# A transformer block on one core: banks per copying engine at the beginning, weights by another queue, bias additions and last transposes in other slots

## The chip, the cores and the metric

The kernel runs on one core of a Trainium2 chip. The metric is the device time of one execution in microseconds (us). A core has TensorE (matmuls and transposes), VectorE, ScalarE, GpSimd and SyncE; each works through its own list of instructions in order, and they wait for each other by semaphores. DMAs are issued from the list of an engine (here SyncE's and ScalarE's) and carried out by 16 DMA engines. TensorE writes to PSUM[...]; the other engines copy results from there into SBUF.

## The reference

A transformer block in float32 on x of 2 × 1024 × 256 with a context of 2 × 154 × 192:

```python
h = _layernorm(x, ln1_g, ln1_b)
x = _attention(h, h, sa_wq, sa_wk, sa_wv, sa_wo, sa_bo) + x        # 16 heads of 64
h = _layernorm(x, ln2_g, ln2_b)
x = _attention(h, cond_emb, ca_wq, ca_wk, ca_wv, ca_wo, ca_bo) + x
h = _layernorm(x, ln3_g, ln3_b)
p = h @ ff_w1 + ff_b1
a, gate = (p[..., :D_FF], p[..., D_FF:])                            # D_FF = 1024
h = a * jax.nn.gelu(gate, approximate=False) @ ff_w2 + ff_b2
return h + x
```

`_attention` projects queries, keys and values with heads side by side, takes the softmax of q·k/8 along the keys, weighs the values with it, and multiplies by the output weights, with the bias added.

## The kernel before, in words

**Stages.** The 16 heads are taken in 8 pairs, so there are 16 units of (batch, pair). After a beginning the work is written out by hand as a row of slots: 128 self-attention slots (loop at L991, variable `p`, 8 per unit), 48 cross-attention slots (loop at L1012, variable `c`, 3 per unit), and 64 slots of the gated feed-forward. No planner moves anything: each engine gets its instructions in the order in which the loops emit them.

**A self-attention slot** takes 128 query rows for both heads of the pair. `self_first` computes two tiles of scores (L445, 16 matmuls each) into PSUM, VectorE takes their maxima (L606), ScalarE the exponents (L456, four instructions). The keys of a row lie in two halves on different partitions, so maxima and sums of the halves are exchanged: `exchange` issues four DMAs of 1 KB from SyncE's queue (L466). In the next slot, `join` (L474 to L482) lets GpSimd and ScalarE put the halves together, VectorE takes the reciprocal (L553), and GpSimd scales the exponents (L557, four instructions). `turn_groups` (L571) lets VectorE transpose them, two slots after their scores.

**What lies beside it in a slot.** In order: the scores, stored copies from the slot before, exponents, transposes, additions of output tiles (`adds`), the scaling, one entry of the list `later` (L1009: loads of x, of weights, single bias additions on GpSimd at L288), `load_ahead` (L640: weight slices for the unit after next), and then TensorE work. Slots 0, 1, 4 and 5 of a unit take this from `run_work`: the projections of queries, keys and values of the next unit (L330, L355), output tiles (L423), norm pieces. Slots 2, 3, 6 and 7 multiply values (`self_values`, L492).

**PSUM** has three pools: two buffers of two banks for scores, two single banks (`mm_tile`) for projections and output tiles, and two single banks for sums (`sum_tile`).

**The beginning** (L944 to L980) normalises the first batch in four pairs of row tiles: statistics on VectorE, the power −0.5 on GpSimd (L220), the normalisation on ScalarE (L240, two per pair), four transposes of a pair into one bank (L247), and four copies out of it with gain and shift. For pairs one and three VectorE makes all copies (L257), for pairs two and four VectorE makes two and ScalarE two (L261). Queries and keys of the first unit are projected in halves of two pairs each, and ScalarE copies them (L340, L344). Ahead of and between these TensorE transposes the identity into an unused bank 32, 10 and 4 times (L959).

**Weight slices.** `load_slice` (L123) issues them on SyncE's queue: a slice of queries, keys or values of self-attention is two DMAs of 128 KB. `load_ahead` asks for them in slots 2 (queries), 3 (keys) and 7 (values) of a unit, in unit 0 in slots 5, 6 and 7. Of the cross-attention's weights it loads the first.

**Bias additions.** `add_biases` puts eight additions and one load into `later`, at the start of units 4 and 6 for the self-attention's bias, so that each of eight slots from slot 0 on takes one.

**Output tiles.** `out_piece` (L418) multiplies 128 rows of one half of the pairs (four matmuls) and VectorE adds the result to x (L430). From unit 4 on, two such tiles are due in each unit, in an order that takes tiles 3 and 7 last; those of batch 1, first half, are due in units 12 to 15.

**The end of self-attention.** `self_drain` (L654) runs in cross slots 0 to 4: the scaling of slot 127 in slot 0, the transposes of slots 126 and 127 in cross slots 0 and 1. The values of the last slots are multiplied in cross slots 3 and 4. A cross slot computes scores (L733), their maxima on VectorE (L738), exponents on ScalarE (L749), scaling on GpSimd (L760) and transposes on VectorE (L776).

Of the kernel before, what the change touches and what calls it, by code (L numbers as in the profile page):

```python
# [13 lines left out]
P = 128  # L14
# [4 lines left out]
def tile_transformer_block(ctx: ExitStack, tc: tile.TileContext, a: dict, out: bass.AP):  # L19
# [103 lines left out]
    def load_slice(name, c0, n, p):  # L123

        own = w[name][:, c0:c0 + n]
        if p != HR:
            return load_rows(wpool, name[3:], f"{name}_{c0}", own, p)
        t = wpool.tile([P, NH, n], F32, tag=name[3:], name=f"{name}_{c0}")
        for r0 in range(0, P, HR):
            nc.sync.dma_start(out=t[r0:r0 + HR], in_=own.rearrange("(c p) f -> p c f", p=HR))  # L130
        return t
# [3 lines left out]
    def load_weights(kind, pr, what):  # L135
        if kind == "sa" or what == "q" or what == "k":
            wsl[kind, pr, what] = load_slice(
                f"{kind}_w{what}", pr * P, P, HR if kind == "sa" or what == "q" else CC)
        elif pr % 2 == 0:
            wsl[kind, pr, what] = load_slice(f"{kind}_w{what}", pr * P, VC, CC)  # L140
# [50 lines left out]
    def norm_pieces(kind, b, first=False):  # L191
# [31 lines left out]
        def normalize(t):  # L223
# [9 lines left out]
            for i in range(2):  # L233
                xs = xt[b, order[t + i] // GT][:, order[t + i] % GT, :]
                xs, own = xs.rearrange("p (c d) -> p c d", c=nh), xn[:, :, i, :]
                if kind == "ca" and not narrow(kind, b):
# [6 lines left out]
        def turn(t):  # L243
            ph = spare["bank"](f"ph_{ln}_{b}_{t}").rearrange("p (c k) -> p c k", c=nh)
            for i in range(2 * D // P):

                nc.tensor.transpose(  # L247
                    ph.rearrange("p c k -> p (c k)")[:, i * P:(i + 1) * P],
                    st["xn", t].rearrange("p c i d -> p (c i d)")[:, i * P:(i + 1) * P], ident)

            def store():
                k = NC * 2 * P // nh
                for c in range(nh):
                    own = st["hT"][:, c, t // 2 * k:(t // 2 + 1) * k]
                    gain, shift = cols[:, g0 + c:g0 + c + 1], cols[:, b0 + c:b0 + c + 1]
                    if first and (c < nh // 2 or t % 4 == 0):
                        nc.vector.tensor_scalar(  # L257
                            own, ph[:, c, :], gain, shift, op0=ALU.mult, op1=ALU.add
                        )
                    else:  # L260
                        nc.scalar.activation(  # L261
                            own, ph[:, c, :], AF.Identity, bias=shift, scale=gain
                        )
# [59 lines left out]
    def project_both(dst, pq, wt, h, m, t0=0, n=S // 2, mul=None):  # L323
# [12 lines left out]
        def store():  # L336
            for r in range(2):
                k0, own = r * S // 2 + t0, pq[r][:, t0:t0 + n]
                if mul is not None:
                    nc.scalar.activation(dst[:, k0:k0 + n], own, AF.Copy, scale=mul)  # L340
                    continue

                dk = dst.rearrange("p (h n j) -> p n h j", h=2, j=KB)
                nc.scalar.copy(  # L344
                    dk[:, k0 // QG:(k0 + n) // QG], own.rearrange("p (n h j) -> p n h j", h=2, j=KB))

        return store
# [29 lines left out]

    def self_pieces(b, pr, parts=1):

        t = {}
        first = (b, pr) == (0, 0)

        def start():
            t["h"] = hT["sa", b]
            t["q"] = p2.tile([P, S], F32, tag="QT", name=f"q_sa{b}_{pr}")
            t["k"] = p2.tile([P, S], F32, tag="KT", name=f"k_sa{b}_{pr}")
            t["v"] = pt_.tile([P, NT, 2, P], F32, tag="V", name=f"v_sa{b}_{pr}")  # L390
            qk["sa", b, pr] = (t["q"], t["k"], t["v"])

        def qk_part(what, i):
            n = S // 4 if first else S // 2
            if what == "q" and i == 0:
                start()
            if not first or (what, i) == ("q", 1):
                t["bank"] = two_banks(f"p{what}_sa{b}_{pr}_{i}")
            elif i == 0:
                own = ps_s.tile([P, 2, HB], F32, tag="s", name=f"p{what}_first")  # L400
                t["bank"] = [own[:, r, :] for r in range(2)]
                t["bank", what] = t["bank"]
            else:
                t["bank"] = t["bank", what]
            return project_both(
                t[what], t["bank"], wsl["sa", pr, what], t["h"], P if first else KB, i * n, n,
                scale if what == "q" else None)

        def v(i):
            n = GT // parts  # L410
            return project_self_values(
                t["v"], two_banks(f"pv_sa{b}_{pr}_{i}"), wsl["sa", pr, "v"], t["h"], i * n, n)

        return [
            costing(2, lambda what=what, i=i: qk_part(what, i)) for what in "qk" for i in range(1 + first)
        ] + [costing(2, lambda i=i: v(i)) for i in range(parts)]
# [202 lines left out]
    def self_beside(ui):  # L619
# [9 lines left out]
        if ui >= HP:  # L629
# [10 lines left out]
    def load_ahead(p):  # L640

        ui, n = divmod(p, 2 * SH)
        for what in "qkv":
            at = {"q": 2, "k": 3, "v": 2 * SH - 1}[what] + 3 * (ui == 0 and what != "v")
            if n != at:
                continue
            if ui + 2 < NU:
                load_weights("sa", units[ui + 2][1], what)
            elif ui + 2 == NU or what == "q":
                load_weights("ca", units[ui + 2 - NU][1], what)  # L650
        if p == SA - 2:
            load_weights("ca", units[1][1], "k")

    def self_drain(p):  # L654
# [3 lines left out]
        if p - LAG < SA:  # L658
            turn_groups(p - LAG)
# [6 lines left out]
    def cross_pieces(b, pr, m=P):  # L666
# [3 lines left out]
        def q():  # L670
# [3 lines left out]
            return project_both(  # L674
# [437 lines left out]
```

## Time and profile before

| what | value |
|---|---|
| three runs | 1160.11, 1154.67, 1160.47 us; median 1160.11 |
| profiled execution | 1154.65 us, its span 1152.6 us, TensorE clock 1.0 |
| TensorE busy | 1124.7 us, 98% of the span |
| VectorE busy | 833.9 us, 72% |
| ScalarE busy | 650.3 us, 56% |
| GpSimd busy | 670.5 us, 58% |
| DMA | 59.92 MB, mean 52 GB/s |
| first scores | 20.21 us |
| self-attention slots | 20 to 729 us |
| one reduction / one transpose on VectorE | 1.22 / 1.22 us, two of each per slot |
| one scaling on GpSimd | 0.77 us, four per slot |
| one bias addition on GpSimd | 0.73 us |

The profiled execution is one run with the hardware profiler on; its span is the time between its first and last instruction. Matmuls are pipelined and their ends are modelled, so the sums of TensorE are a little rough. In the views of the profile, a row of the timeline gives start, length, engine, line and operation, written tile, read tiles, their shapes and the number of instructions, and in brackets the idle time of the engine ahead of it with what ended it. The view of waits gives which engine at which line waited for what, how long in total, how often and the longest. The chain of waits follows back from the last instruction to what released it at each step. "L456" is line 456 of the kernel before; queues of an engine are written SPq, ACTq.

### The profile page before, as it was taken

What the parts mean: (1) busy time and instruction counts of PE and PEld (TensorE: products, weight loads), DVE (VectorE), ACT (ScalarE), POOL (GpSimd) and SP (SyncE); (2) the same over time, 40 slices, a digit from 0 to 9 for tenths busy, and PEclk for the clock granted to TensorE, in tenths of its full rate; (3) what the DMA queues carried; (4) which work ended last, traced back from release to release, by engine and by line L of the source; (5) the groups of instructions that cost most, each with busy time, mean ns of one, the idle gap of its engine ahead of it and who ended that gap; (6) DMA issues with size and microseconds to landing.
All of it is one profiled execution on the core that took longest, in us unless ns stands there. A gap on an engine that the chain in (4) does not pass through costs nothing.

```text
span 1152.6 us, 36693 instructions
## 1 busy us (share of the span) xinstructions
PE 1124.7 (98%) x14343; PEld 683.3 (59%) x14343; DVE 833.9 (72%) x1184; ACT 650.3 (56%) x2085; POOL 670.5 (58%) x1564
## 2 busy tenths in 40 slices
PE   8989999999999999999999999999999999999998
PEld 6434444545545545545455454566666667888887
DVE  4779898889888989999998889657666664232222
ACT  5656666767666665666677666646755571041111
POOL 1767777877887777777777777647654453020000
PEclk9999999999999999999999999999999999999999
DMA  2331111111111111111011010167544433000000
GB/s 78 77 93 40 30 31 39 31 31 39 31 35 40 28 33 40 29 32 40 22 40 39 22 32 12 44 146 195 148 121 117 117 83 68 10 11 10 19 10 18
DMA packets 104733, 59.92 MB, mean 52 GB/s; under 512 B 31914, under 2 KB 95346, under 8 KB 104562
## 3 DMA queue, kind: packets, MB, share of 16 engines
q1 hardware_dynamic: 101202, 54.84, 20.0%
q10 hardware_dynamic: 3360, 2.76, 0.8%
q8 instruction: 113, 1.85, 0.7%
q14 instruction: 58, 0.48, 0.1%
HBM read 27.91 MB, written 2.10 MB: 26 GB/s over the span
## 4 chain that ended last, share of the span: by engine, by line
PE 83%; ACT 5%; POOL 4%; DVE 2%; issue 2%; DMA 2%; SPq 1%; DVEq 0%; ACTq 0%; POOLq 0%
PE po L492 16%; PE s L445 16%; PE pa L899 10%; PE py_ca L423 5%; PE py_sa L423 5%; PE pf L922 5%; PE pq_ca L330 5%; PE pk_sa L330 4%; PE poc L812 4%; PE pv_sa L355 4%; PE pq_sa L330 4%; ACT p L456 4%; PE sc L733 3%; DMA st<-st 2%; DVE st L606 2%
## 5 line engine op out<-in xcount | busy, mean ns | idle before, releaser
L456 ACT ACTIVATE p<-s,st 128x512 f32<-128x512 f32 x512 | 344.8, 685 | 201.9 <-DVE st L606 193.8
L557 POOL TENSOR_SCALAR p<-p,rd,ee 128x512 f32<-128x512 f32 x512 | 385.6, 767 | 44.8 <-DVE rd L553 43.7
L606 DVE TENSOR_REDUCE st<-s 128x2 f32<-128x1024 f32 x256 | 301.3, 1218 | 37.5 <-PE s L445 22.6
L571 DVE STREAM_TRANSPOSE pT<-p 128x1024 f32<-128x1024 f32 x256 | 302.3, 1218 | 2.5 <-POOL p L557 2.5
L445 PE MATMUL s<-k_sa,q_sa 64*32 64x512 f32 x4096 | 254.4, 595 | 13.2 <-ACT p L456 12.2
L492 PE MATMUL po<-pT,v_sa 64*64 64x256 f32 x4096 | 235.8, 379 | 0.0
L492 PEld LDWEIGHTS po<-pT,v_sa 64*64 64x64 f32 x4096 | 150.5, 133 | 109.1 <-issue 35.3
L760 POOL TENSOR_SCALAR p<-p,rden 128x154 f32<-128x154 f32 x256 | 96.8, 398 | 98.6 <-DVE rden L757 98.1
L445 PEld LDWEIGHTS s<-k_sa,q_sa 64*32 64x32 f32 x4096 | 64.9, 106 | 139.0 <-issue 65.2
L749 ACT ACTIVATE p<-sc,neg 128x154 f32<-128x154 f32 x256 | 95.9, 396 | 80.2 <-DVE rden L757 76.1
L899 PE MATMUL pa<-hT_ln,wf 128*128 128x256 f32 x512 | 121.0, 379 | 0.0
L908 DVE SCALAR_TENSOR_TENSOR u<-pa,cols,gate 128x256 f32<-128x256 f32 x64 | 30.9, 484 | 124.4 <-ACT gate L905 124.4
L905 ACT ACTIVATE gate<-pa,cols 128x256 f32<-128x256 f32 x64 | 30.3, 473 | 151.5 <-PE pa L899 151.5
L899 PEld LDWEIGHTS pa<-hT_ln,wf 128*128 128x128 f32 x512 | 96.8, 190 | 13.7 <-issue 0.4
L456 ACT ACTIVATION_READ_ACCUMULATOR p<-s,st 128x1 f32 x512 | 103.8, 203 | 0.0
L738 DVE TENSOR_REDUCE neg<-sc 128x6 f32<-128x924 f32 (+1 forms) x48 | 48.5, 1010 | 43.2 <-PE sc L733 43.2
L355 PEld LDWEIGHTS pv_sa<-sa_wv,hT_ln 64*128 64x128 f32 x1024 | 59.0, 188 | 17.8 <-DMA st<-st 7.5
L480 POOL TENSOR_TENSOR zz<-ee,st 128x8 f32<-128x8 f32 x128 | 25.9, 202 | 68.7 <-ACT ee L478 68.7
L922 PE MATMUL pf<-wf,u 128*128 128x256 f32 x256 | 65.0, 379 | 0.2 <-DVE u L908 0.2
L355 PE MATMUL pv_sa<-sa_wv,hT_ln 64*128 64x128 f32 x1024 | 62.8, 276 | 1.0 <-ACT v_sa L364 1.0
L423 PE MATMUL py_ca<-ca_wo,o_ca 128*128 128x256 f32 x256 | 60.8, 384 | 0.3 <-ACT hT_ln L261 0.3
L330 PE MATMUL pq_ca<-hT_ln,ca_wq 64*128 64x512 f32 (+1 forms) x304 | 60.5, 591 | 0.2 <-ACT hT_ln L261 0.2
(81 smaller groups left out, 1247.3 us busy)
## 6 DMA issues: line engine op xcount, KB each, us to landing
wf<-pT_ca SPq DMA_DIRECT2D x128, 128.0 KB, 2.5
st<-st SPq DMA_DIRECT2D x512, 1.0 KB, 1.8
v_sa<-v_sa SPq DMA_DIRECT2D x32, 256.0 KB
sa_wq<-in_L_xattn_sa_wq_dram SPq DMA_DIRECT2D x32, 128.0 KB, 3.0
sa_wk<-in_L_xattn_sa_wk_dram SPq DMA_DIRECT2D x32, 128.0 KB, 3.5
sa_wv<-in_L_xattn_sa_wv_dram SPq DMA_DIRECT2D x32, 128.0 KB, 2.9
ca_wq<-in_L_xattn_ca_wq_dram SPq DMA_DIRECT2D x32, 128.0 KB, 2.8
wf<-in_L_xattn_ff_w_dram SPq DMA_DIRECT2D x12, 256.0 KB, 2.9
```

Of the source, the lines that this page charges most:

```text
L330: nc.tensor.matmul(pq[r][f:f + m, t0:t0 + n], lhsT=wt[own, c, f:f + m], rhs=h[own, c, t0:t0 + n], start=(c == 0), stop=(c == NH - 1), tile ...
L355: nc.tensor.matmul(pv[r][:, i * P:(i + 1) * P], lhsT=h[own, c, i * P:(i + 1) * P], rhs=wt[own, c, :], start=(c == 0), stop=(c == NH - 1), ...
L423: nc.tensor.matmul(py[:, :D], lhsT=o[:, i, t * P:(t + 1) * P], rhs=wo[kind][:, half * HP + i, :], start=(i == 0), stop=(i == HP - 1),)
L445: nc.tensor.matmul(sc[a4 * KB:(a4 + 1) * KB, j, :], lhsT=q[r, c:c + KB], rhs=k[r, h * HB:(h + 1) * HB], start=True, stop=True, tile_positi ...
L456: nc.scalar.activation(pr[:, j, :], sc[:, j, :], AF.Exp, bias=st[:, 0, 0, i, j:j + 1], accum_out=st[:, 0, 1, i, j:j + 1],)
L492: nc.tensor.matmul(po[a2][j * DH:(j + 1) * DH, :QH // 2], lhsT=v[r, t, e, j * DH:(j + 1) * DH], rhs=pT[r, j * NK + n, :], start=(t == 0 an ...
L557: nc.gpsimd.tensor_scalar(pr[:, j, :], pr[:, j, :], rd[:, c:c + 1], ee[:, 0, c:c + 1], op0=ALU.mult, op1=ALU.mult,)
L571: nc.vector.transpose(halves[h][:, :, c:c + KB], groups.pop(0).rearrange("p j (n k) -> p (j n) k", k=KB))
L606: nc.vector.tensor_reduce(st[:, 0, 0, i, :], sc[i], AX.X, ALU.max, negate=True)
L760: nc.gpsimd.tensor_scalar(pr_[:, j, i, :T], pr_[:, j, i, :T], rden[:, j, i:i + 1], 1.0, op0=ALU.mult, op1=ALU.mult,)
L899: nc.tensor.matmul(pa[:, half, :TF * P], lhsT=w1[:, c, half * DF + f * P:half * DF + (f + 1) * P], rhs=h[:, c, t0 * P:(t0 + TF) * P], star ...
L922: nc.tensor.matmul(sums[blk][i][:, :D], lhsT=sums[blk, "u"][:, f, i * P:(i + 1) * P], rhs=w2[:, f, :], start=(f == 0), stop=(f == NF - 1),)
```

## The change

It has five parts.

- The beginning: each pair's four transposes go to two banks, two to each, VectorE copies from one and ScalarE from the other. Of the two normalisations of a pair the second goes to GpSimd. Queries of the first two pairs and keys of all four are projected pair by pair (128 columns each) in the banks of the two score buffers. Of the two copies of the keys the second is made by VectorE. The warming transposes are 27, at the start only.
- Weight slices from `load_ahead` are issued on ScalarE's queue, queries in slot 3, keys in slot 6 and values in slot 7 of a unit (unit 0: 5, 6, 7 as before).
- `later` gives nothing in slots 0 and 1 of a unit from unit 1 on, so the bias additions that were there come in slots 2 and 3 of the next unit.
- Unit 15 has no output tiles: those of tiles 3 and 7 of batch 1, first half, become due in cross slot 1 and are computed in cross slots 1 and 2.
- The transposes of slot 127 move from cross slot 1 to cross slot 2.

The core of the diff (projection and its copies become two functions, `project_both` and `take_both`; the pieces of a unit are regrouped without other effect):

```diff
-    def load_slice(name, c0, n, p):
+    def load_slice(name, c0, n, p, queue):
...
-            nc.sync.dma_start(out=t[r0:r0 + HR], in_=own.rearrange("(c p) f -> p c f", p=HR))
+            queue.dma_start(out=t[r0:r0 + HR], in_=own.rearrange("(c p) f -> p c f", p=HR))
...
-                if kind == "ca" and not narrow(kind, b):
+                if kind == "ca" and not narrow(kind, b) or first and i == 1:
                     nc.gpsimd.tensor_scalar(
...
-            ph = spare["bank"](f"ph_{ln}_{b}_{t}").rearrange("p (c k) -> p c k", c=nh)
+
+            n = 2 if first else 1
+            bank = mm_tile if first and t % 4 else spare["bank"]
+            ph = [bank(f"ph_{ln}_{b}_{t}_{i}") for i in range(n)]
...
-                    if first and (c < nh // 2 or t % 4 == 0):
+                    if first and c < nh // 2:
                         nc.vector.tensor_scalar(
...
+    def take_both(dst, pq, mul=None, t0=0, n=S // 2, shared=False):
+
+        for r in range(2):
+            k0, own = r * S // 2 + t0, pq[r][:, t0:t0 + n]
+            if mul is not None:
+                nc.scalar.activation(dst[:, k0:k0 + n], own, AF.Copy, scale=mul)
+                continue
+
+            dk = dst.rearrange("p (h n j) -> p n h j", h=2, j=KB)[:, k0 // QG:(k0 + n) // QG]
+            own = own.rearrange("p (n h j) -> p n h j", h=2, j=KB)
+            if shared and r:
+                nc.vector.tensor_copy(dk, own)
+            else:
+                nc.scalar.copy(dk, own)
...
-        if ui >= HP:
+        if HP <= ui < NU - 1:
             ob, oh = divmod((ui - HP) // HP, 2)
...
-            at = {"q": 2, "k": 3, "v": 2 * SH - 1}[what] + 3 * (ui == 0 and what != "v")
+            at = {"q": SH + 1 if ui == 0 else SH - 1, "k": 2 * SH - 2, "v": 2 * SH - 1}[what]
...
-                load_weights("sa", units[ui + 2][1], what)
-            elif ui + 2 == NU or what == "q":
-                load_weights("ca", units[ui + 2 - NU][1], what)
-        if p == SA - 2:
-            load_weights("ca", units[1][1], "k")
+                load_weights("sa", units[ui + 2][1], what, nc.scalar)
+            elif ui + 2 == NU or what != "v":
+                load_weights("ca", units[ui + 2 - NU][1], what, nc.scalar)
...
-        if p - LAG < SA:
-            turn_groups(p - LAG)
+        if p == SA or p == SA + LAG:
+            turn_groups(p - LAG if p == SA else SA - 1)
...
-        busy(32)
+        for _ in range(27):
+            nc.tensor.transpose(pk[:, 0, :P], ident, ident)
         emit(stats[0], stats[1], deviation[0])
-        emit(stats[2], normalize[0], stats[3], deviation[1])
-        copies = turn[0]()
-        busy(10)
-        emit(stats[4], normalize[1])
+        emit(stats[2], stats[3], normalize[0], deviation[1], stats[4], normalize[1])
+        copies = [turn[0](), turn[1]()]
+        copies[0]()
+        part("q", 0)
+        part("k", 0)
+        emit(stats[5], deviation[2])
+        copies[1]()
+        emit(stats[6], normalize[2], stats[7], deviation[3])
+        part("q", 1)
+        copies = turn[2]()
+        part("k", 1)
         copies()
-        emit(stats[5], deviation[2])
-        copies = turn[1]()
-        busy(4)
+        emit(normalize[3])
+        take("q", 0)
+        take("k", 0)
+        copies = turn[3]()
+        part("k", 2)
         copies()
-        emit(normalize[2], stats[6], stats[7], deviation[3])
-        q_copy, copies = q0(), turn[2]()
-        emit(normalize[3])
-        q_copy()
-        copies()
-        k_copy, copies = k0(), turn[3]()
-        k_copy()
-        copies()
-        emit(k1)
+        part("k", 3)
+        take("k", 2)
...
-            if later:
+            if later and (p < 2 * SH or p % (2 * SH) > 1):
                 later.pop(0)()
...
+            if c == 1:
+                out_pieces("sa", B - 1, 0, tile_order("ca")[NT - 2:])
```

Here `part(what, i)` projects pair i of the first unit's queries or keys, and `take(what, i)` copies pairs i and i + 1, the second half of the keys' columns by VectorE.

## The prediction

> **What bounds the kernel now.** I read the busy time by stretch first, since one average over three stages with different limits says little. Columns: the stretch, its length, then busy us of TensorE, weight loads, VectorE, ScalarE, GpSimd.
>
> ```profile
> 20.20:67.00 46.80, 43.95 (x721) 22.52 (x729) 33.70 (x36) 29.45 (x88) 25.13 (x60) 1.00 0.31 76
> 67.00:80.00 13.00, 10.05 (x176) 3.16 (x160) 9.66 (x11) 7.81 (x22) 8.02 (x19) 1.00 0.38 103
> ...
> 290.00:684.00 394.00, 394.00 (x6516) 206.70 (x6507) 356.03 (x398) 260.93 (x766) 296.66 (x664) 1.00 0.15 33
> ...
> 706.00:735.00 29.00, 24.31 (x316) 12.60 (x302) 25.66 (x29) 19.12 (x70) 22.61 (x51) 1.00 0.13 33
> 735.00:791.00 56.00, 56.00 (x484) 36.75 (x482) 33.88 (x76) 28.26 (x131) 30.18 (x84) 1.00 0.53 132
> ```
>
> From 290 to 684 and again from 735 to 791 TensorE is busy without a gap, at full clock. There an edit counts only if it takes matmuls away. Idle TensorE exists at the beginning, in 20–290 (about 13 us, counted over these stretches and those between) and before the cross slots: 29.00 − 24.31 = 4.7 us. All five parts touch these places.
>
> The waits, in us in total, times, longest, show what the copying and loading parts could reach:
>
> ```profile
> ACT p L456 <- DVE st L606: 193.8, 118, 2.6
> ...
> POOL dd L474 <- DMA st<-st: 52.6, 48, 16.4
> ```
>
> The first is ScalarE's idle time in a stage that TensorE bounds: free. Of the second, 16.4 us are the first slot's, before there was anything to do, and most others are under 1 us. Only two matter, GpSimd's 2.81 us at 65.09 and this one, read in the order of time with the chain of waits beside it:
>
> ```profile
> 73.02 0.20 POOL L474 TENSOR_TENSOR dd<-st 128x4 f32<-128x4 f32 x1 [3.11 <-DMA st<-st]
> ```
> ```profile
> 66.58 6.22 DMA st<-st
> ```
>
> The exchange of slot 7 landed 6.22 us after its last issue (median 1.8).
>
> [...]
>
> ```profile
> 11.07 0.72 DVE L257 TENSOR_SCALAR hT_ln<-ph_ln,cols 128x128 f32<-128x128 f32 x2
> ...
> 11.88 0.81 ACT L261 ACTIVATE hT_ln<-ph_ln,cols 128x128 f32<-128x128 f32 x2 [2.38 <-issue]
> ...
> 20.21 1.09 PE L445 MATMUL s<-k_sa,q_sa 64*32 64x512 f32 x16 [0.74 <-ACT k_sa L344]
> ```
>
> ScalarE was free for 2.38 us and began its half of the second pair only at 11.88, after VectorE's half ended at 11.79.
>
> [...] sa_wo, 1 MB, was issued on ScalarE's queue at 65.82, and the exchange on SyncE's queue landed at 72.8 with it.
>
> **The change, part by part.** Sums stand against the profiled execution (1154.65 us, span 1152.6). The median of the three runs is 1160.11, 5.46 above; I add the same difference to it.
>
> *A, the beginning.* First scores now start at 20.21. With a bank for each engine, a pair's copies run beside each other: 0.81 us in place of 0.72 + 0.81 for pairs two and four (the VectorE-only pairs took 1.36). Half of the normalisations go to GpSimd, 0.55 us by its rows of line 237 beside 0.55 on ScalarE, where ScalarE took 1.09. VectorE's copy of half of the keys has no row; I take ScalarE's 0.33, and the bounds below are wide enough for 0.2 or 0.5. Against this stand four projections of a pair in place of two of two pairs, about 1.0 us each by the 2.00 us of one with twice the columns, and the 27 warming transposes, which end at about 7.5 by the rate of the present 32 (6.66 us). Laying the new order out by hand with these durations, and 0.70 us for GpSimd's power, gives the first scores at about 19.35: −0.9. Bounds: 0, if copies stay in sequence, and −1.6, if everything overlaps. The later half's second query projection and the values move with it and are unchanged. [...]
>
> *B, weights on ScalarE's queue.* The loads' 45 issues leave SyncE (about 0.63 us each) and come to ScalarE (0.37 us by sa_wo's). ScalarE has 394 − 261 = 133 us idle in 290–684, 2.7 us per slot, and what these DMAs wait for ended a slot before: issuing is free, and the exponents behind are not held, since they wait for VectorE anyway. On SyncE the exchange followed the last exponent by 0.15 us in nearly every slot, but by 0.58 and 1.0 in slots 6 and 7. So only these gain. Slots 7 and 8 took 7.18 and 7.93 us, about 5.3 being usual: 4.5 us too much. But sa_wo remains and is issued at 65.8; an exchange issued 0.85 us earlier still has its last part beside it. I take −1; bounds −3 and 0. Against it, weights now come in slots 3, 6, 7 of a unit, right beside the exchange, 128 KB each twice at most. The page has 128 KB landing in 3.0 us and the 1 KB exchange in 1.8, so the data take about 1.2 us; the exchange has 0.8 to 1.0 us of slack in the bound slots (GpSimd is busy with the scaling before it needs the pieces), and units 1 to 3 also copy values (512 KB) in slot 6. I take +1, bounds 0 and +2 outside the rival below. B: 0.
>
> *C, no biases in slots 0 and 1.* Such slots last 5.47 us in unit 6 (4 scalings of 0.753, the joins, and 0.73 for the bias: GpSimd is the longest) and 5.15 in unit 8. Unit 6 takes 44.03 us, units 7 to 10 take 43.45. So −0.58 there, and about −0.3 in unit 4, which has other waits. The four moved additions go to slots 2 and 3 of units 5 and 7, where TensorE's own 5.5 us covers 5.47; without that cover 0.3 us each. C: −0.8, bounds −1.2 and −0.3.
>
> *D and E, out-projections and last transposes.* Tiles 3 and 7 of the first half of batch 1 leave slot 121 and come to cross slots 1 and 2: 16 matmuls, 3.72 us. Slots 121 to 123 last 5.53, 5.49, 5.49 by TensorE's work; VectorE's two reductions and two transposes (5.05) become the limit. So 3.65 us of matmuls leave but only about 0.5 + 0.45 + 0.4 = −1.36 is gained. Later this work is paid again, where the chain of waits now reads (start, length):
>
> ```profile
> 731.77 2.22 ACT p L749 x12
> 733.99 0.19 ACT k_ca L684
> 734.18 0.04 issue
> 734.22 1.06 PE sc L733 x12
> 735.28 3.43 PE pq_ca L330 x16
> 738.71 3.38 PE po L492 x57
> ```
>
> TensorE waits at most 1.37 us there, ahead of the scores at 734.22. Tile 3 (1.83 us) fills that gap and overruns it; the other 3.65 − 1.37 = 2.3 us lengthen the path. The second price is a wait. VectorE gets the last transposes (2 × 1.2) ahead of the addition of tile 7, and the query projection of cross slot 3 takes that tile's bank. VectorE's line: addition of tile 3, reduction 0.76 until about 735.5, where it ended at 736.75 behind the transposes (what E is for: ScalarE's next exponents start 1.2 us earlier, but the path does not pass through them), transposes until 737.85, cross transposes 1.19 until 739.05, addition 0.42 until 739.5. The projection's second bank starts there, not at 735.3, and it ends about 742.6 in place of 738.71: +3.9 in all, so that the wait alone is 1.6. Behind it on TensorE stand the last value products, in a stretch without a gap (735–791), so nothing gives it back. D and E: −1.36 + 3.9 = +2.5; bounds +1 (if the addition gets ahead) and +3.5.
>
> Sum: −0.9 + 0 − 0.8 + 2.5 = +0.8. Profiled 1155.5, runs 1160.11 + 0.8 = 1160.9.
>
> **Rivals.**
> 1. *The banks don't help.* The second key copy is VectorE's, the destination tile is shared with ScalarE's, and in the program VectorE's copy waits for ScalarE's; the last projection and the scores wait for that. For: two copies take 0.65 us in a row now too (19.51), so nothing is saved at the end. Against: the pairs' copies still overlap. A = 0: 1161.8.
> 2. *Slower: weights beside the exchange.* If the exchange's small packets queue behind 256 KB on the same engines, they land 1.2 us later; past 0.8 us of slack it is 0.4 us for GpSimd, VectorE and then TensorE, in 3 slots of 13 units: 0.4 × 39 = 15.6, so about +15: 1176. It decides once exchanges in slots 3, 6, 7 land over 1 us later than now. For: the 6.22 us above. Against: weights already come in slots 2, 3, 7, and in 290–684 TensorE never waits.
> 3. *Faster: the early stall goes.* Slots 7 and 8 give back 4.5 us, units 2 to 5 another 2, C 0.8, A 0.9, and the transition costs 0.5 since VectorE's addition arrives in time: −7.7, 1152.4. For: units 1 to 5 stand 0.75 to 1.65 us each above 43.45. Against: sa_wo stays where it was.
>
> **How the numbers follow.** Likeliest 0.54; rival 1 0.22; rival 2 0.13; rival 3 0.11. About 0.5%, 5.8 us, is what a measurement can tell from no change: the runs before themselves lie at 1154.67 and at 1160.11 to 1160.47. So the likeliest and rival 1 are no change (0.76), rival 2 slower (0.13), rival 3 faster (0.11). Range: the bounds of the parts, −1.6 − 3 − 1.2 + 1 = −4.8 and 0 + 2 − 0.3 + 3.5 = +5.2, widened to rival 3 at the low end (1152.5) and by about a part of rival 2, 2 us, at the high end (1167).
>
> **What would show it.** A: ScalarE's pair copies start with VectorE's, first scores near 19.4. B: no loading issue ahead of an exchange on SyncE; slots 7 and 8 still long, at about 7. C: units 4 and 6 near 44.7 and 43.5. D and E: slots 121 to 123 at 5.05 to 5.1, a TensorE wait of over 1 us for VectorE's addition of tile 7 before the second bank of the cross slot's query projection, and the stretch from 690 to 742 longer by 2.5. Wrong if slots 7 and 8 fall to 5.3, or if TensorE shows gaps in 290–684.

## The result and the profile after

The changed kernel takes 1161.73 us by the median of 20 runs (1158.67 to 1163.91), the kernel before 1157.94 us by 20 runs (1154.41 to 1160.47). The ratio is 1.0038 (95% interval 1.0027 to 1.0050), so about 4.4 us slower (3.1 to 5.8), just inside what the forecast called no change. Its +0.8 us was right in direction and too small by some 3.6 us. The profiled execution has a span of 1159.0 us against 1152.6. The profile before is of one of that kernel's shortest runs (1154.65 us) at a full clock, so the 6.4 us between the profiles are more than the 4.4 of the runs.

The stretches of the forecast again, in the kernel after (stretch, length, then busy us of TensorE, weight loads, VectorE, ScalarE, GpSimd, clock, DMA share, GB/s):

```profile
20.20:67.00 46.80, 44.63 (x745) 22.67 (x729) 36.61 (x38) 29.49 (x89) 28.19 (x63) 1.00 0.36 94
67.00:80.00 13.00, 10.26 (x176) 4.00 (x172) 8.94 (x11) 8.85 (x25) 7.43 (x18) 1.00 0.19 40
290.00:684.00 394.00, 393.81 (x6468) 209.18 (x6456) 354.27 (x397) 259.39 (x762) 296.44 (x658) 1.00 0.15 33
706.00:735.00 29.00, 24.97 (x321) 12.59 (x318) 24.96 (x29) 18.39 (x64) 21.09 (x49) 1.00 0.12 28
735.00:791.00 56.00, 55.09 (x474) 36.28 (x473) 30.37 (x65) 25.68 (x121) 26.94 (x74) 1.00 0.43 114
```

TensorE still looks busy in 290 to 684, yet these 394 us hold 6468 matmuls and held 6516 (over the whole self-attention both traces hold all the matmuls of scores and values): the records stretch over short waits, so a full row does not prove that nothing waits. One row of the waits before, then the waits of the kernel after:

```profile
PEld s L445 <- ACT p L456: 54.7, 89, 2.2
```
```profile
ACT p L456 <- DVE st L606: 156.8, 115, 3.0
...
PEld s L445 <- ACT p L456: 65.7, 100, 3.5
...
POOL dd L474 <- DMA st<-st: 51.5, 43, 14.0
```

The row of L445 tells it: the weight loads of the score matmuls waited 65.7 us for ScalarE's exponents (54.7 before). ScalarE's own wait for the maxima fell from 193.8 to 156.8, and what is new in its list behind the beginning are the DMA issues.

Where the 6.4 us of the two profiles lie is read from the starts of VectorE's maxima (L606, then those of the cross slots) in the timeline, in us:

| stretch | before | after | SyncE's queue again | A alone | A and C | tiles in sum banks | A, C, sa_wo in parts |
|---|---|---|---|---|---|---|---|
| to the first maxima | 21.4 | 20.1 | 20.2 | 20.2 | 20.4 | 20.2 | 20.3 |
| slots 0 to 7 | 45.5 | 43.8 | 45.3 | 45.7 | 46.3 | 44.2 | 45.8 |
| slots 8 to 15 | 45.0 | 47.2 | 44.7 | 47.1 | 50.3 | 48.6 | 43.9 |
| slots 16 to 119 | 572.3 | 575.7 | 570.9 | 572.2 | 571.1 | 576.0 | 572.3 |
| slot 120 to the first cross maxima | 42.0 | 42.0 | 42.8 | 41.8 | 41.8 | 42.9 | 41.9 |
| first to seventh cross maxima | 27.1 | 31.0 | 31.0 | 28.9 | 28.9 | 29.0 | 28.7 |
| the rest | 399.2 | 399.3 | 399.2 | 399.2 | 399.2 | 399.3 | 399.3 |

(The further columns are kernels told of below.) The rest is the same to 0.1 us everywhere. Before that, the kernel after has gained 1.3 us at the beginning and 1.7 in slots 0 to 7, and lost 5.6 in slots 8 to 119 and 3.9 in the cross slots. The granted clock is 1.00 in all these stretches of before and after. Other columns were granted less in places: A and C 0.91 from 20 to 40 us, 0.80 from 74 to 90 and 0.89 from 735 to 750, the last one 0.91 from 20 to 40 and 0.88 from 722 to 735. A alone and the sum banks had a mean of 0.997 over the whole execution. By my estimate (0.20 of 16 us is 3.2, 0.12 of 13 us is 1.6) differences of 1 to 3 us between columns there may be the clock's.

The beginning, after. ScalarE's copies of pairs two to four now start beside VectorE's; the keys' copies follow each other:

```profile
13.09 0.73 DVE L261 TENSOR_SCALAR hT_ln<-ph_ln,cols 128x128 f32<-128x128 f32 x2 [1.17 <-PE ph_ln L250]
...
13.30 0.81 ACT L265 ACTIVATE hT_ln<-ph_ln,cols 128x128 f32<-128x128 f32 x2 [1.51 <-PE ph_ln L250]
...
18.02 0.37 ACT L351 COPY k_sa<-pk_first 128x256 f32<-128x256 f32 x1 [1.81 <-PE pk_first L332]
18.43 0.42 DVE L349 COPY k_sa<-pk_first 128x256 f32<-128x256 f32 x1 [1.93 <-ACT k_sa L351]
18.90 0.18 PEld L445 LDWEIGHTS s<-k_sa,q_sa 64*32 64x32 f32 x16 [1.12 <-DVE k_sa L349]
```

The transition, after: the chain of waits (start, length), and the matmuls of the query projection in the timeline:

```profile
737.46 2.25 POOL p L759 x6
739.71 0.08 POOL p L744
739.79 0.04 issue
739.84 1.20 DVE pT_ca L775 x2
741.03 0.32 DVE x L430
741.35 0.04 issue
741.39 3.70 PE pq_ca L332 x14
```
```profile
739.46 1.02 PE L332 MATMUL pq_ca<-hT_ln,ca_wq 64*128 64x512 f32 x2
741.39 3.70 PE L332 MATMUL pq_ca<-hT_ln,ca_wq 64*128 64x512 f32 x14 [0.91 <-DVE x L430]
```

That is the forecast's second price in place: TensorE begins the projection, then waits (0.91 us here, where the forecast said over 1) until VectorE has added tile 7 behind all its transposes.

### The profile page after: what moved, and what is told of

It reads as the page before. It is cut to its first block, busy times and chain, and to the rows that moved or that the text cites. A ratio compares the mean times of both kernels' runs of the same rounds, so it can differ in the third digit from the quotient of the medians.

```text
span 1159.0 us, 36675 instructions
## 1 busy us (share of the span) xinstructions
PE 1127.1 (97%) x14372; PEld 686.1 (59%) x14372; DVE 833.1 (72%) x1182; ACT 650.7 (56%) x2083; POOL 676.3 (58%) x1568
## 4 chain that ended last, share of the span: by engine, by line
PE 75%; ACT 8%; DMA 4%; DVE 4%; POOL 4%; issue 2%; SPq 2%; DVEq 0%; ACTq 0%; POOLq 0%
PE s L445 14%; PE po L492 13%; PE pa L898 10%; ACT p L456 6%; PE py_ca L423 5%; PE pf L921 5%; PE py_sa L423 4%; PE pq_ca L332 4%; DMA st<-st 4%; PE pk_sa L332 4%; PE poc L811 4%; PE pv_sa L359 4%; PE sc L732 3%; PE pq_sa L332 3%; DVE st L606 3%
## 5 line engine op out<-in xcount | busy, mean ns | idle before, releaser
L456 ACT ACTIVATE p<-s,st 128x512 f32<-128x512 f32 x512 | 345.2, 687 | 170.0 <-DVE st L606 156.8
L557 POOL TENSOR_SCALAR p<-p,rd,ee 128x512 f32<-128x512 f32 x512 | 387.7, 773 | 45.1 <-DVE rd L553 43.2
L606 DVE TENSOR_REDUCE st<-s 128x2 f32<-128x1024 f32 x256 | 301.3, 1218 | 31.2 <-PE s L445 22.8
L445 PE MATMUL s<-k_sa,q_sa 64*32 64x512 f32 x4096 | 256.5, 595 | 18.3 <-ACT p L456 17.1
L445 PEld LDWEIGHTS s<-k_sa,q_sa 64*32 64x32 f32 x4096 | 66.0, 106 | 144.1 <-ACT p L456 65.7
L737 DVE TENSOR_REDUCE neg<-sc 128x6 f32<-128x924 f32 (+1 forms) x48 | 48.5, 1011 | 46.4 <-PE sc L732 46.4
```

The costliest lines, as they stand in the source:

```text
L445: nc.tensor.matmul(sc[a4 * KB:(a4 + 1) * KB, j, :], lhsT=q[r, c:c + KB], rhs=k[r, h * HB:(h + 1) * HB], start=True, stop=True, tile_positi ...
L456: nc.scalar.activation(pr[:, j, :], sc[:, j, :], AF.Exp, bias=st[:, 0, 0, i, j:j + 1], accum_out=st[:, 0, 1, i, j:j + 1],)
L557: nc.gpsimd.tensor_scalar(pr[:, j, :], pr[:, j, :], rd[:, c:c + 1], ee[:, 0, c:c + 1], op0=ALU.mult, op1=ALU.mult,)
L606: nc.vector.tensor_reduce(st[:, 0, 0, i, :], sc[i], AX.X, ALU.max, negate=True)
```

## The experiments

Each ratio is to the kernel before, run on the same chip with it, with its 95% interval. "Queue" is the name for part B below.

**1. Is it the queue, the slots or the bias additions?** Three kernels differ from the changed one only in the weight slices.

```diff
-                load_weights("sa", units[ui + 2][1], what, nc.scalar)
+                load_weights("sa", units[ui + 2][1], what)
...
-                load_weights("ca", units[ui + 2 - NU][1], what, nc.scalar)
+                load_weights("ca", units[ui + 2 - NU][1], what)
```

> The changed kernel, but with the weight slices of load_ahead on SyncE's queue again, at the changed kernel's slots 3, 6 and 7. In the changed kernel the slots from 8 to 120 take 5.6 us more than before, and exchanges land later. Theory: on ScalarE's queue the slices are issued at the same time as the four exchange DMAs and share the DMA engines with them, on SyncE's queue they stand behind them. Then nearly all of that goes: 4 to 6 us less than the changed kernel, about 1156.5 to 1157.5 by the median of 20 runs, and the median landing of an exchange is back near 1.8 us from 2.5. Rival: it is the slots, 6 and 7 next to each other with the copies of values; then it stays within 1.5 us of the changed kernel, 1160 to 1163. Second rival: it is the bias additions in slots 2 and 3; then it stays as well, and so does the next kernel.

Measured: 1157.06 us, 0.9994 (0.9985 to 1.0003). So 0.0044, 5.1 us (about 3.4 to 6.8), hang on the queue, at these slots. In the profiles slots 16 to 119 fall by 4.7 us and slots 8 to 15 by 2.5, while slots 0 to 7 take 1.5 more (table). Most of the 4.7 us lies in the first slots of the units: 5.45 us with ScalarE's queue and 5.22 with SyncE's (means of units 2 to 14), where GpSimd waits 0.56 and 0.28 us for the exchange of slot 7. The median landing of an exchange, over the some 50 of 512 exchange DMAs whose landing the trace has, is 1.8 us in the kernel with SyncE's queue; in the kernel after it is 2.5. The lines of the page, after and then with SyncE's queue, and the waits of the latter:

```profile
st<-st SPq DMA_DIRECT2D x512, 1.0 KB, 2.5
```
```profile
st<-st SPq DMA_DIRECT2D x512, 1.0 KB, 1.8
```
```profile
PEld s L445 <- ACT p L456: 56.6, 88, 3.5
POOL dd L474 <- DMA st<-st: 47.0, 42, 14.2
```

The slices fully as before (queue and slots; of this edit the line of the slots is shown, the rest puts the cross-attention's first loads back):

```diff
-            at = {"q": SH + 1 if ui == 0 else SH - 1, "k": 2 * SH - 2, "v": 2 * SH - 1}[what]
+            at = {"q": 2, "k": 3, "v": 2 * SH - 1}[what] + 3 * (ui == 0 and what != "v")
```

> The changed kernel with the weight slices fully as before: SyncE's queue and slots 2, 3 and 7. Theory (queue): the same as the kernel with SyncE's queue and the new slots, 4 to 6 us below the changed kernel. Rival (slots): only this one is 4 to 6 us lower, the other not. Rival (bias additions): neither is lower.

Measured: 1157.81 us, 0.9994 (0.9983 to 1.0006). On SyncE's queue the slots make no difference that can be told, and the bias additions were in slots 2 and 3 in both kernels; both rivals fall as causes of their own. Then the old slots on ScalarE's queue:

> The changed kernel with the weight slices on ScalarE's queue but at the old slots 2, 3 and 7. The queue alone is back to SyncE in the kernel that had SyncE's queue at the new slots, and it lay 5 us below the changed one. Theory (the queue lets the slices start beside the exchange, whatever the slot): as slow as the changed kernel, 1161 to 1163, with a median landing of the exchange of about 2.5 us. Rival (queue and slot together, since slots 6 and 7 follow each other): about half of the loss goes, 1159; landing about 2.2.

Measured: 1160.53 us, 1.0016 (1.0005 to 1.0027): half of the loss. The rival was right here: the queue costs 0.0022 at the old slots and 0.0044 at the new ones. The median landing is 1.8 us, so this figure from few records does not follow the loss, and nothing below rests on it.

**2. Shared DMA engines or ScalarE's own time?** Every self-attention slice is loaded once more, into a tile that nothing reads; first on ScalarE's queue, in the changed kernel.

```diff
                 load_weights("sa", units[ui + 2][1], what, nc.scalar)
+                extra = wpool.tile([P, NH, P], F32, tag="extra", name=f"extra_{p}")
+                c0 = units[ui + 2][1] * P
+                for r0 in range(0, P, HR):
+                    nc.scalar.dma_start(
+                        out=extra[r0:r0 + HR],
+                        in_=w[f"sa_w{what}"][:, c0:c0 + P].rearrange("(c p) f -> p c f", p=HR))
```

> The changed kernel with every self-attention slice of load_ahead on ScalarE's queue loaded once more into a tile that nothing reads, so that twice the bytes go beside the exchanges of slots 3, 6 and 7. Theory (shared DMA engines): the loss of 5 us at least doubles, since the slack is used up, 1167 to 1180, and slots 3, 4, 7 and 0 of a unit grow. Rival (ScalarE's queue costs its engine's issue time): 84 more issues of 0.63 us where ScalarE waits 2.7 us a slot, less than 2 us more, 1162 to 1164.

Measured: 1195.1 us, 1.0302 (1.0276 to 1.0329). The size is the theory's and more, but the place in the trace is the rival's. In this kernel's timeline, ScalarE in a slot 0:

```profile
489.69 2.07 ACTq L130 DMA_DIRECT2D sa_wv<-in_L_xattn_sa_wv_dram  x2
491.85 1.48 ACTq L652 DMA_DIRECT2D extra<-in_L_xattn_sa_wv_dram  x2
493.38 0.65 ACT L591 COPY o_sa<-po 128x256 f32<-128x256 f32 x2 [3.49 <-DMA sa_wv<-in_L_xattn_sa_wv_dram]
493.91 0.70 ACT L456 ACTIVATE p<-s,st 128x512 f32<-128x512 f32 x1
```

Four issues hold ScalarE's list for 3.6 us, the copy and the exponents behind them come late. From the start of the maxima to that of the exponents it took 1.26 us in nearly every slot of the kernel before; here 2.62 in slot 0 of a unit, 2.09 in slot 4 and 1.84 in slot 7 (means of units 1 to 14). That is 1.36 + 0.83 + 0.58 = 2.8 us per unit, 39 us in 14 units, enough for the 33.4 us between the medians (30.6 by the ratios). The theory's way is there too: GpSimd's waits for the exchanges of slots 3 and 6 rise from 0.45 and 0.43 us in the changed kernel to 0.77 and 1.03. My rival had the main mechanism and took the slack for enough. The same bytes on SyncE's queue, in the kernel of the first experiment (the same lines with `nc.sync`):

> The changed kernel with the slices on SyncE's queue at the new slots, and every self-attention slice loaded once more on SyncE's queue into a tile that nothing reads. On ScalarE's queue the same extra bytes cost 33 us (1195.1 against 1161.7). Theory (on SyncE's queue the slices stand behind the exchange of their slot): much less than on ScalarE's queue, at most 12 us above the kernel without the extra loads (1157.1), because only their own issue time (84 of 0.63 us, two or four to a slot) can run into the next exchange. Rival (bytes near the exchange cost the same on either queue): 1185 to 1195.

Measured: 1172.64 us, 1.0128 (1.0104 to 1.0151), 15.6 us above that kernel without them. Less than half of the cost on ScalarE, but above my ceiling of 12. Exponents are at 1.26 us in nearly every slot; GpSimd instead waits for the exchanges of slots 7 and 0, by a mean of 1.0 us each (0.26 and 0.32 without the extra loads). Its join follows the last exchange issue by 1.89 and 1.78 us there, no later than without the extra loads (1.88 and 1.90), so it is the issues themselves that come late: SyncE's list is now the full one.

In the changed kernel itself the holding of ScalarE shows once, in slot 8:

```profile
63.93 2.36 ACTq L130 DMA_DIRECT2D sa_wv<-in_L_xattn_sa_wv_dram  x1
66.33 0.65 ACT L591 COPY o_sa<-po 128x256 f32<-128x256 f32 x2 [3.33 <-issue]
66.87 0.70 ACT L456 ACTIVATE p<-s,st 128x512 f32<-128x512 f32 x1
```

One issue took 2.36 us there (median 0.63), beside sa_wo on the same queue, and the exponents began 1.7 us late. In nearly all other slots they keep 1.26 us, as before. What remains of the 5 us goes with later exchanges: GpSimd's join follows the last exchange issue by 2.16, 2.24 and 2.27 us in slots 3, 6 and 7, and by 2.03, 1.94 and 1.88 with SyncE's queue (means of units 1 to 14). So both costs are there. How the rest divides between data on the DMA engines and the issue times was not separated.

**3. Output tiles and last transposes.** Both put back in the changed kernel:

```diff
-        if HP <= ui < NU - 1:
+        if ui >= HP:
...
-        if p == SA or p == SA + LAG:
-            turn_groups(p - LAG if p == SA else SA - 1)
+        if p - LAG < SA:
+            turn_groups(p - LAG)
...
-            if c == 1:
-                out_pieces("sa", B - 1, 0, tile_order("ca")[NT - 2:])
```

> The changed kernel with output tiles 3 and 7 back in slot 121 and the last transposes back in cross slot 1. Theory: the transition from slot 121 to the value products of cross slot 3 is 2.5 us shorter (1.0 to 1.4 us more in slots 121 to 123, 3.7 us less in cross slots 1 to 3), and the whole 2.5 us lower than the changed kernel, 1159.2. Rival: what the slots 121 to 127 lost to other waits (1.2 us were lost again in slots 124 to 126) was chance, so the gain in them is the full price and the whole is only 1 us lower or less.

Measured: 1159.34 us, 1.0005 (0.9993 to 1.0017): 0.0033, 3.8 us less than the changed kernel (about 1.9 to 5.7; 2.4 by the medians). A second pair gives nearly the same: SyncE's queue at the old slots with D and E (0.9994) stands 0.0035 above A and C without them (0.9959, fourth experiment). The same kernels compared the other way give the queue once more: 1.0005 against 0.9959 is 0.0046 without D and E, 0.0044 with them.

So D and E cost 3.8 us by the runs, where the forecast said 2.5. The 3.9 us in the cross slots are there between the profiles before and after; what failed is the gain. Slots 121 to 126 together take 31.9 us before and with A alone, 32.4 here, and with the tiles moved 32.1 (after) and 33.0 (SyncE's queue). In the kernel after, slots 121 to 123 did fall, from 16.5 to 15.5 us, and slots 121 and 122 to the forecast's 5.05. But slots 124 to 126 took 16.6 in place of 15.4: in slots 124 and 126 GpSimd waited 1.02 and 1.21 us for the exchange and VectorE 0.58 and 0.85 us for GpSimd's sums, which they did not before. TensorE in the kernel after, and then with SyncE's queue:

```profile
694.59 1.09 PE L445 MATMUL s<-k_sa,q_sa 64*32 64x512 f32 x16 [2.61 <-ACT p L456]
695.92 1.09 PE L445 MATMUL s<-k_sa,q_sa 64*32 64x512 f32 x16 [0.25 <-ACT p L456]
696.95 3.68 PE L492 MATMUL po<-pT,v_sa 64*64 64x256 f32 x64
```

```profile
688.86 1.09 PE L445 MATMUL s<-k_sa,q_sa 64*32 64x512 f32 x16 [2.60 <-ACT p L456]
690.20 1.96 PE L445 MATMUL s<-k_sa,q_sa 64*32 64x512 f32 x16 [0.24 <-ACT p L456]
692.09 4.26 PE L492 MATMUL po<-pT,v_sa 64*64 64x256 f32 x64
```

Without the tiles, TensorE waits 2.6 us in both for a score buffer to be freed by the exponents, ahead of the scores of slot 122: it can't run ahead, and most of the 3.65 us taken away became idle time. With SyncE's queue the matmuls behind this wait were slower: the second 16 take 1.96 us in place of 1.09, the 64 of the values 4.26 in place of 3.68, and slot 122 takes 6.4 us. Slot 122 took 6.0 to 6.4 us in three more of the eight profiles with D and E.

Without D and E a lower clock was granted in the cross slots: 0.63 from 737 to 745 us in the kernel of this experiment, 0.89 and 0.88 with A and C and in the last column of the table (735 to 750 and 722 to 735 us). In the kernel of this experiment:

```profile
731.85 0.95 PE L732 MATMUL sc<-k_ca,q_ca 64*128 64x154 f32 x12
737.30 1.91 PE L732 MATMUL sc<-k_ca,q_ca 64*128 64x154 f32 x12 [1.86 <-ACT k_ca L683]
```

Its stretch from the first to the seventh cross maxima takes 30.0 us, 28.7 to 28.9 with A alone, with A and C, and in the last column of the table, and 27.1 only in the profile before, at a full clock (1.00 from 726 to 757 us). In the kernel after it is 31.0, at 1.00 too. So against these profiles the moved work costs 1.0 to 2.3 us there and not 3.9, and the price of D and E is not the same in every execution.

The bank wait by itself: the tiles stay in the cross slots but get the sum pool's banks there.

```diff
-            spare["out"] = mm_tile if i < n else sum_tile
+            spare["out"] = mm_tile if i < n and not own else sum_tile
...
-            run_work(2, 1, n_sum=2 * (SH < c < 2 * NPAIR and c % len(CG) == 0))
+            run_work(2, 1, n_sum=2 * (SH < c < 2 * NPAIR and c % len(CG) == 0), own=c < len(CG))
```

> The changed kernel with output tiles 3 and 7 of cross slots 1 and 2 in the sum pool's banks, so that the query projection of cross slot 3 has no bank to wait for; the work stays. Theory: the stretch from the first to the seventh maxima of the cross slots falls from 30.99 us by the wait, 1.3 to 1.9 us, to about 29.4, and the time to about 1160.2. Rival: the wait is only the visible end of VectorE's chain (the query tile's reader, the value products behind the last transposes), and another wait takes its place: under 0.5 us less.

Measured: 1159.88 us, 1.0013 (0.9997 to 1.0029), and in the profile 28.98 us in place of 30.99 between the first and the seventh cross maxima: the wait is worth 2.0 us there. By the runs it is 0.0025, with an uncertainty of 0.0020. TensorE goes on without a gap:

```profile
741.83 1.06 PE L732 MATMUL sc<-k_ca,q_ca 64*128 64x154 f32 x12
742.72 3.60 PE L332 MATMUL pq_ca<-hT_ln,ca_wq 64*128 64x512 f32 x16
```

**4. The beginning and the bias additions.** The kernel before with the changed beginning alone:

> The kernel before with the changed beginning alone. Theory: first maxima at 20.1 in place of 21.4 as in the changed kernel, and nothing later to take it back, so 1.3 us below the kernel before (1156.6 against 1157.9 by the median of 20 runs). Rival: GpSimd or DMA work of the first slots takes it back, since slots 7 and 8 wait for an exchange beside the load of sa_wo: 0.

Measured: 1155.31 us, 0.9980 (0.9969 to 0.9990): 2.3 us less (1.2 to 3.6). First maxima are at 20.2, as in after. Then C as well, which is this line in the loop:

```diff
-            if later:
+            if later and (p < 2 * SH or p % (2 * SH) > 1):
```

> The kernel before with the changed beginning and with no entries of later in slots 0 and 1 of a unit. The changed beginning alone gave 0.998 of the kernel before. Theory: units 4 and 6 lose 0.3 to 0.6 us each, so 0.8 to 1.5 us less than with the beginning alone, about 0.997. Rival: the slots of these units are held by other waits, and the additions cost as much where they come later: 0.998 again, with unit 6 at 44.0.

Measured: 1154.56 us, 0.9959 (0.9943 to 0.9976). And C undone in the changed kernel:

> The changed kernel, but later gives its entries in every slot again, so that the bias additions are back in slots 0 and 1. Theory (C is a gain of 0.8 us, as forecast, or up to 2.4 as the kernel with the beginning and C stood to the one with the beginning alone): 0.8 to 2.4 us above the changed kernel, 1162.5 to 1164. Rival: C costs nothing and gains nothing beside the slices on ScalarE's queue, since those slots wait for exchanges: 1161 to 1162.

Measured: 1164.44 us, 1.0056 (1.0038 to 1.0075). C is worth 0.0021 and 0.0018 in the two places, some 2 us, each with an uncertainty as large. Unit 6, where I put most of it, takes 44.0 us in the kernel before, with A alone and with A and C; so do units 11 and 12 of the kernel before, which have no bias additions. Unit 4 takes 45.1 (before) and 46.4 (A alone) without C and 44.2 with A and C; but with ScalarE's queue it takes 45.1 (after) and 46.3 (old slots) with C and 46.4 without. Where C gains is open.

**5. A version that beats both.** A and C, with sa_wo in four parts on SyncE's queue:

```diff
+    def load_out_part(kind, i):
+        if i == 0:
+            wo[kind] = const.tile([P, 2 * HP, D], F32, tag="wo", name=kind + "_wo")
+        nc.sync.dma_start(
+            out=wo[kind][:, 2 * i:2 * i + 2, :],
+            in_=w[kind + "_wo"][2 * i * P:(2 * i + 2) * P, :].rearrange("(c p) f -> p c f", p=P))
...
-        later.append(lambda: load_out("sa", nc.scalar))
+        later.append(lambda: None)
+        later.extend(lambda i=i: load_out_part("sa", i) for i in range(4))
```

> The kernel before with the changed beginning, no entries of later in slots 0 and 1, and the load of sa_wo in four parts of 256 KB on SyncE's queue in slots 10 to 13 in place of one of 1 MB on ScalarE's queue in slot 7. The kernel with the first two alone had 0.9959 of the kernel before. Theory: the exchange of slot 7 no longer lands beside 1 MB, slots 7 and 8 fall from 15 us together to 11, TensorE has no long gap there and so no half-clock stretch behind it (0.80 granted from 74 to 90 us in that profile): 4 us less at least, 1149 to 1151, and a smaller spread over runs. Rival (the parts disturb the exchanges of four slots instead): within 1.5 us, 1153 to 1156.

Measured: 1153.63 us, 0.9953 (0.9938 to 0.9968). The theory's place was right, its size was not: slot 8 falls from 9.4 to 5.0 us, slot 7 only from 7.2 to 6.9, and against A and C in one chunk (0.9959) the difference can't be told from none. The profile of A and C is of the longest of its nine runs (1159.99 us), so 9.4 us is no typical slot 8 (8.05 with A alone, 7.9 before). What differs beside slots 7 and 8 between these two profiles is the stretch at a lower clock. The same two stretches in the profiles of A and C, then of this kernel:

```profile
66.00:74.00 8.00, 5.30 (x96) 1.19 (x80) 4.81 (x5) 3.43 (x10) 3.31 (x6) 0.97 0.63 164
74.00:90.00 16.00, 14.26 (x212) 7.00 (x216) 11.41 (x13) 8.36 (x24) 11.02 (x26) 0.80 0.03 3
```
```profile
66.00:74.00 8.00, 7.72 (x144) 3.07 (x136) 7.69 (x8) 5.47 (x16) 6.88 (x13) 1.00 0.14 36
74.00:90.00 16.00, 15.76 (x287) 8.62 (x273) 14.48 (x16) 10.41 (x32) 12.04 (x28) 1.00 0.16 36
```

The runs of this kernel lie between 1151.57 and 1154.92 (11 runs), those of A and C between 1151.39 and 1159.99 (9 runs). Last, tile 3 alone moved to cross slot 1, in a sum bank, to fill TensorE's gap there:

```diff
-            out_pieces("sa", ob, oh, tile_order("ca")[t0:t0 + 2])
+            out_pieces("sa", ob, oh, tile_order("ca")[t0 + (ui == NU - 1):t0 + 2])
...
+            if c == 1:
+                out_pieces("sa", B - 1, 0, tile_order("ca")[NT - 2:NT - 1])
```

> The same with output tile 3 (not 7) of batch 1, first half, moved from slot 121 to cross slot 1 and into the sum pool's bank, so that TensorE's gap of 1.37 us ahead of the third cross scores is filled. Theory: 1.83 us of work in a gap of 1.37 costs 0.5 us, and the half-clock stretch that follows the gap in some executions (7.14 or 8.18 in place of 5.48 us between the fourth and fifth maxima) goes, so 0 to 1.5 us less than the same kernel without it. Rival: slot 121's work gives nothing back and the clock is lost elsewhere: 0.5 to 1 us more.

Measured: 1151.77 us, 0.9945 (0.9927 to 0.9963), the lowest of all, but not separable from the one before it. In its profile the time between the fourth and fifth cross maxima is 5.10 us (6.96 without the move), and slots 124 to 126 take 18.6 (15.5), with a clock of 0.84 from 690 to 722 us (1.00): in that execution, the longest of its nine, the loss only changed its place.

## Why the forecast was nearly right, and where it was not

- **A** was called −0.9. The first scores came at 18.9 and not 19.35, −1.3, and the runs give −2.3 (1.2 to 3.6). The mechanism held for the pairs' copies (pair three's begin at 13.09 and 13.30 us); for the keys rival 1 described what happened: a second copy of 0.42 us that waits for the first, and TensorE waits for it (0.93 us ahead of the first scores). It did not take the gain away.
- **B** was called 0, with bounds of −3 and +2, and this is the step that failed: "issuing is free, and the exponents behind are not held". The queue costs 5.1 us (first experiment). I took ScalarE's idle time for slack, and mis-sized both sides. The 133 us over the 72 slots of 290 to 684 are 1.8 us per slot and not 2.7, and the loads are 88 issues in the trace after, two per slice, and not 45. Nor is idle time free at the moment of the issue: the copy of value products and the next exponents stand behind the issue in the list. The doubled loads show how that becomes the bound (3.6 us of issues in a slot 0); in the changed kernel itself it shows in slot 8 only. The rest goes with later exchanges, and why they come later was not settled. Rival 2 named later exchanges with a price of 15 us; a third of it came, and not by that way alone. "In 290–684 TensorE never waits", set against it, read the full row for more than it shows: the weight loads of the scores waited 11.0 us in that stretch before, and 16.8 after. The gain of 1 us in slots 7 and 8 did not come either: 14.9 us, 15.1 before (slot 7 fell by 0.9, slot 8 rose by 0.7).
- **C** was called −0.8, with −0.58 in unit 6. Unit 6 gained nothing: it was set against units 7 to 10, and what makes it longer than these isn't the additions, since units 11 and 12 are as long without any. The whole gained about 2 us with an uncertainty as large; unit 4 fell by 2.2 us from A alone to A and C, but it varies by as much with C in place.
- **D and E** were called −1.36 + 3.9. The second term is 3.9 between the two profiles, and its bank wait, called 1.6, measured 2.0; against the profiles without D and E that had a lower clock in the cross slots (0.63 to 0.89), the term is 1.0 to 2.3. The first term came in its place (slots 121 to 123, −1.0 us in the kernel after) and was lost again within three slots, to waits for the exchange, or, with SyncE's queue, to slower matmuls behind TensorE's wait of 2.6 us (1.96 us in place of 1.09). The forecast added it as if nothing behind could take it back. By the runs D and E cost 3.8 us (1.9 to 5.7), which doesn't exclude the 2.5.

By the runs, −2.3 + 5.1 − 2 + 3.8 = +4.6, against +4.4 measured. Against the forecast's terms the errors are −1.4, +5.1, −1.2 and +1.3. That they cancelled down to 3.8 us, so that "no change" came true, is luck and no merit of the terms: B alone nearly fills the 5.8 us that the forecast could tell from no change.

## What to carry to other kernels

A DMA that is moved to another engine's queue takes a place in that engine's list (here, with the doubled loads, four issues held ScalarE's list for 3.6 us, with the copy and the exponents behind them): ask what stands behind it in that list at that moment, not how idle the engine is over a slot. Work taken out of a busy slot gives time only if the engine can run ahead into it and nothing in the slots behind takes the time back (here 3.65 us of matmuls left and TensorE waited 2.6 us for a score buffer); count the buffers between it and its consumer first. And look where a moved piece's bank or buffer is wanted next: here a tile of 1.8 us held a projection for 2.0 us more, and another free bank took that away.

## What the runs showed of the hardware

Behind a wait of TensorE the granted clock was lower in some executions, and the matmuls took longer. With A and C TensorE waited 3.85 us in slot 8, and 0.80 of the clock was granted from 74 to 90 us: the first 40 matmuls behind the wait took 4.85 us, where 57 of the same projection took 3.72 in the kernels before and after. The longest waits there in these two, 2.38 and 1.37 us, were followed by 1.00. In the kernel without D and E waits of 1.14 and 1.86 us were followed by 0.63 from 737 to 745 us: twelve matmuls of the cross scores took 1.91 us, and 0.95 ahead of the waits. The waits of 2.61 and 2.60 us ahead of slot 122 were followed by 1.00 in the kernel after (694 to 698 us, 16 matmuls in 1.09 us) and, with SyncE's queue, by 16 matmuls in 1.09 us and the next 16 in 1.96. So in these executions the length of a wait alone did not decide what came behind it; what does, no run here settles.

The granted clock shows in the measured times: of the 67 runs of the kernel before in the first set of experiments, the 8 with a mean clock of 1.0 took 1155.5 us on average, the 26 with 0.997 took 1159.6. The time of a DMA issue isn't fixed either: 0.63 us is the median on ScalarE's queue, and 2.36 us was seen beside 1 MB on it.
